# A planner that treats GpSimd and two-operand VectorE work as exclusive, and that waits for work due sooner

## The chip, the core and the metric

The kernel runs on one core of a Trainium2 chip. The metric is device time in microseconds (us), the median of several runs. Five engines run side by side, each through its own queue in order: the tensor engine (PE, with its weight loads PEld), VectorE (DVE), ScalarE (ACT), GpSimd (POOL) and SyncE (SP), which issues the loads and stores here. They wait for each other by semaphores.

## What is computed

One transformer block with normalization behind each half, in float32, for two sequences of 512 tokens of width 512. Attention has 32 query heads and 8 key heads of 128, so that four query heads share a key head; a feed-forward network of inner width 1376 with integer weights and scales per column follows.

```python
q = _rmsnorm((x @ Wq.T).reshape(b, s, 32, 128).transpose(0, 2, 1, 3), q_norm_w)
k = _rmsnorm((x @ Wk.T).reshape(b, s, 8, 128).transpose(0, 2, 1, 3), k_norm_w)
v = (x @ Wv.T).reshape(b, s, 8, 128).transpose(0, 2, 1, 3)
scores = jnp.einsum('bkgqd,bksd->bkgqs', qg, k) / math.sqrt(HD)
bias = jnp.where(rel > 0, NEG_INF, slopes[:, :, None, None] * rel)
attn = jax.nn.softmax(scores + bias[None], axis=-1)
out = jnp.einsum('bkgqs,bksd->bkgqd', attn, v)   # heads joined, then @ Wo.T
x = _layernorm(x + attention(x))
h = silu((x @ gate_w.T) * gate_s) * ((x @ up_w.T) * up_s)
x = _layernorm(x + (h @ down_w.T) * down_s)
```

## The kernel before

**Two halves of a program.** The function post_ln_block does not emit instructions as it goes. It describes operations with `W.add`: their possible engines with a price in us for each (costs), a due time (prio, smaller is sooner), the buffers read and written, and a function that emits the instructions. At the end `W.emit` walks through a simulated time and emits all operations in one order. That order is the program order of each engine's queue, and it also fixes which engine takes an operation that can go to several. Buffers come from rings; an operation that opens a new buffer has to wait in the plan until the users of the buffer it replaces have finished. LAG is what the plan adds from the end of an operation to its visibility on another engine.

**How it chooses.** Before, each step looked at every ready operation on every engine that it may use and took the smallest of (start, due time, end, number), where start is the later of the operation's readiness and the time at which the engine is free. So an operation that could start a moment earlier went first, however late it was due, and was never held back.

**The prices.** `pe(n)` is n/600 us for n columns; `act(n)`, `dve(n)`, `pool_tt(n)` and `pool_ts(n)` are straight lines in the elements per partition. `dve(n, sbuf=True)`, 0.2 + 0.0014 n, was for VectorE work with two operands in SBUF, 0.15 + 0.00106 n for the rest.

**The stages.** Attention is done in units (g, b, i): key head g, sequence b, block i of 128 query tokens; two units make a pair p, and there are 32 pairs. For pair p, with u = 2p, the due times are:
- u - 3: `sums_q`, the sums of a group's weights (tile tq), and `sums_x` of the input (sx), each four additions or subtractions (`sums_a`, `sums_b`); a matrix product is done with seven block products instead of eight (`seven`), which needs such sums of both factors. `sums_o` does the same for the output weights (to), due at u + 1.
- u - 2.4: `project`, the products for queries, keys and values into PSUM banks pa_q, pb_q, pc_q, and their eviction into c: the first value of a block is copied (ACT or DVE), the next is added (DVE).
- u - 1.8: `heads`: squares on ACT (sq), their sum on DVE (ms), the inverse root on POOL (inv, a power of -0.5 of 128x10 values, line 504), the scaling of q and k with it (sq, DVE or POOL), transposes on PE (ptq, ptk), evictions into qT and kT.
- u + k for unit k of the pair: `scores`: for each of four blocks of 32 queries of the four heads, a product on PE (sc), bias and maximum on DVE (pr, nmax), exp on ACT; then the reciprocal of the sums (rden) and four scalings of pr on POOL (line 924).
- u + k + 0.4: `attend`: transposes of pr (pt), evictions (prT), the product with v (pa), its eviction (aT).
- u + 2.6: `project_out`: four sums of aT (so, 128x256 each), seven products with the output weights (pa_o, pb_o, pc_o), each added to y on DVE.

A group's bias is four operations on POOL. After the last group come the first layernorm and the FFN: integer weights are converted to float (wf), summed (sw), multiplied (pa_h, pb_h, pc_h), and `finish` makes sigmoid (ACT) and two products with three factors each (sg, hT, DVE, lines 1289 and 1298). The down projection uses sums of hT (sh) and of its weights (td) and adds to y; the second layernorm and the store follow.

**Sums by either engine.** The helper `tensor` gives an operation to DVE or POOL where both are allowed. Line 518 is therefore the line of all sums and additions in the trace; their tile tells them apart. Line 566 is that of all seven-product matmuls, 641 and 643 are the copies.

Of the kernel before, what the change touches and what calls it, by code (L numbers as in the profile page):

```python
# [53 lines left out]
def act(n, scaled=False):  # L54
    return 0.15 + 0.00084 * n + (0.1 if scaled else 0.0)


def dve(n, sbuf=False):
    return 0.2 + 0.0014 * n if sbuf else 0.15 + 0.00106 * n


def pool_tt(n):
    return 0.28 + 0.0021 * n


def pool_ts(n):
    return 0.3 + 0.00095 * n


LAG = {"PE": 0.22, "DVE": 0.1, "ACT": 0.12, "POOL": 0.2, "SP": 0.1, "ACTQ": 0.1, "NONE": 0.0}  # L70
TABLE = 1.28


class Ring:
# [21 lines left out]
class Work:  # L96
# [3 lines left out]
        self.ops = []  # L100
        self.wrote, self.read = {}, {}

    def add(self, costs, prio, fn, reads=(), writes=(), after=(), table=None, lag=0.0):

        op = {
            "costs": costs,
            "prio": prio,
            "fn": fn,
            "deps": set(id(o) for o in after),
            "obj": list(after),  # L110
            "takes": [],
            "end": None,
            "table": table,
            "lag": lag,
            "n": len(self.ops),
        }
        deps = {id(o): o for o in after}
        for key in reads:
            o = self.wrote.get(key)
            assert o is not None, (key[0].name, key[1])  # L120
            deps[id(o)] = o
        for key in writes:
            o = self.wrote.get(key)
            if o is not None:
                deps[id(o)] = o
            for o in self.read.get(key, ()):
                deps[id(o)] = o
        for key in reads:
            if key not in writes:
                self.read.setdefault(key, []).append(op)  # L130
        for key in writes:
            self.wrote[key] = op
            self.read[key] = []
        bufs = []
        for key in list(reads) + list(writes):
            b = key[0]
            if b not in bufs:
                bufs.append(b)
        for b in bufs:
            op["takes"].append(b)  # L140
            b.users.append(op)
        op["deps"] = list(deps.values())
        self.ops.append(op)
        return op

    def emit(self):
        ops = self.ops
        left = [len(o["deps"]) for o in ops]
        nexts = [[] for _ in ops]
        for o in ops:  # L150
            for d in o["deps"]:
                nexts[d["n"]].append(o)
        free, table = {}, [None]
        dma = 0.0
        ready = []

        def at(o):
            t = 0.0
            for d in o["deps"]:
                t = max(t, d["end"] + d["lag"])  # L160
            return t

        for o in ops:
            if not left[o["n"]]:
                o["at"] = 0.0
                ready.append(o)
        emitted = 0
        while ready:
            best = None
            for o in ready:  # L170
                t0 = o["at"]
                for b in o["takes"]:
                    if b.tile is not None:
                        continue
                    r = b.ring
                    if r.gate is not None and r.gate["end"] is None:
                        t0 = None
                        break
                    k = len(r.items) - r.bufs
                    if k >= 0:  # L180
                        for u in r.items[k].users:
                            if u["end"] is None:
                                t0 = None
                                break
                            t0 = max(t0, u["end"] + LAG[u["eng"]])
                        if t0 is None:
                            break
                if t0 is None:
                    continue
                for e, c in o["costs"].items():  # L190
                    s = max(t0, free.get(e, 0.0))
                    key = (s, o["prio"], s + c, o["n"])
                    if best is None or key < best[0]:
                        best = (key, o, e, c, s)
            assert best is not None, "no work can start: " + ", ".join(
                b.name for o in ready for b in o["takes"]
            )
            _, o, e, c, s = best
            ready.remove(o)
            if e == "ACT" and o["table"] and o["table"] != table[0]:  # L200
                table[0] = o["table"]
                c += TABLE
            o["eng"] = e
            if e in ("SP", "ACTQ"):
                free[e] = s + 0.45
                dma = max(dma, s + 1.6) + c
                o["end"] = dma + 0.6
            elif e == "NONE":
                o["end"] = s
            else:  # L210
                free[e] = s + c
                o["end"] = s + c
            o["lag"] += LAG[e]
            for b in o["takes"]:
                if b.tile is not None:
                    continue
                b.ring.items.append(b)
                b.tile = b.ring.pool.tile(
                    b.ring.shape, b.ring.dtype, tag=b.ring.name, name=b.name, bufs=b.ring.bufs
                )  # L220
            o["fn"](e)
            emitted += 1
            for x in nexts[o["n"]]:
                left[x["n"]] -= 1
                if not left[x["n"]]:
                    x["at"] = at(x)
                    ready.append(x)
        assert emitted == len(ops)
# [3 lines left out]
def post_ln_block(  # L232
# [278 lines left out]


    def tensor(n, prio, dst, a, b, alu, reads, writes, who=("DVE", "POOL"), sbuf=None, after=()):
        cost = {"DVE": dve(n, len(who) > 1 if sbuf is None else sbuf), "POOL": pool_tt(n)}
        W.add(
            {e: cost[e] for e in who},
            prio,
            lambda e: vec[e].tensor_tensor(dst(), a(), b(), alu),  # L518
            reads,
            writes,  # L520
            after,
        )

    def sums_a(n, prio, s, a, s_key, a_keys):
# [113 lines left out]
    def copy_op(n, prio, dst, src, reads, writes, who=("ACT", "DVE")):  # L638
        def fn(e):
            if e == "ACT":  # L640
                nc.scalar.copy(dst(), src())  # L641
            else:
                vec[e].tensor_copy(dst(), src())  # L643

        cost = {"ACT": act(n), "DVE": dve(n), "POOL": 0.2 + 0.00095 * n}
        W.add({e: cost[e] for e in who}, prio, fn, reads, writes)

    def project_plain(p, prio):
# [393 lines left out]
    def layernorm(t, prio, dst, dst_keys, name):  # L1042
        stats, mv = Buf(r_stats, f"stats_{name}"), Buf(r_mv, f"mv_{name}")
        ve, rstd = Buf(r_ve, f"ve_{name}"), Buf(r_rstd, f"rstd_{name}")
        for n in range(2):
            W.add(
                {"DVE": dve(WO)},
                prio,
                lambda e, n=n: nc.vector.bn_stats(stats[:, n, :], y[:, t, n * WO : (n + 1) * WO]),
                [(y, (t, n))],  # L1050
                [(stats, n)],
            )
        W.add(
            {"DVE": 0.2},
            prio,
            lambda e: nc.vector.bn_aggr(mv.tile, stats.tile),
            [(stats, 0), (stats, 1)],
            [A(mv)],
        )
        W.add(  # L1060
            {"DVE": 0.16},
            prio,
            lambda e: nc.vector.tensor_scalar_add(ve.tile, mv[:, 1:2], LN_EPS),
            [A(mv)],
            [A(ve)],
        )
        rsqrt(lambda: rstd.tile, lambda: ve.tile, 1, prio, A(rstd), A(ve))
        W.add(
            {"DVE": 0.6},
            prio,  # L1070
            lambda e: nc.vector.tensor_scalar(
                dst(), y[:, t, :], mv[:, 0:1], rstd.tile, ALU.subtract, ALU.mult
            ),
            [A(mv), A(rstd), (y, (t, 0)), (y, (t, 1))],
            dst_keys,
        )

    x1T, tx = {}, {}
# [40 lines left out]
    for p in range(NP):  # L1119
        g, b, i = pairs[p]  # L1120
        u = 2 * p
# [100 lines left out]
    def ffn_up(fc, b, weights, prio):  # L1222

        fw = min(P, DFF - fc * P)
        key = f"{fc}_{b}"
# [49 lines left out]
        def finish():  # L1275
# [8 lines left out]
                table="sigmoid",  # L1284
# [6 lines left out]
                ),  # L1291
                [(gu, 0), (gu, 1), A(gs_sb), A(sg)],
                [A(sg)],
            )
            W.add(
                {"DVE": 0.75},
# [8 lines left out]
                ),  # L1305
                [(gu, 2), (gu, 3), A(us_sb), A(sg)],
                [(h, (fc, 0)), (h, (fc, 1))],
            )
            finished.append(W.ops[-1])

# [23 lines left out]
    n = 0  # L1334
# [9 lines left out]
    for fc in range(NF):  # L1344
# [22 lines left out]
            sbuf=True,  # L1367
# [138 lines left out]
```

## Time and profile before

| | |
|---|---|
| median of 3 runs | 1091.03 us (1090.96 to 1091.54) |
| profiled execution, its own time | 1091.2 us |
| its span, first to last instruction | 1089.1 us |
| mean granted clock of the tensor engine | 0.997 |
| instructions | 13052 |
| bytes moved by DMA | 38.92 MB |
| POOL scaling of pr, line 924 | x256, 155.8 us busy, mean 627 ns |
| POOL inverse root, line 504 (inv) | x32, 62.9 us busy, mean 1965 ns |
| DVE sums so from aT, 128x256 | x39, 411 / 428 / 870 ns (least, median, most) |
| DVE sums tq from w and tq, 128x768 | x8, 1039 / 2452 / 2464 ns |
| POOL sums tq from w and tq, 128x768 | x12, 1800 / 1812 / 2415 ns |
| DVE scaling sq, 128x640 | x55, 810 / 825 / 1883 ns |

An engine's busy time is the union of its instructions' records. In the rows above, the least duration is that of an operation which ran undisturbed, the greatest that of one which was held up while it was in its engine. A row of waits reads: who waited, on whom, the total, how often, the longest. A matmul in float32 appears as two records; records overlap, since a matmul is given a start and a modelled end, so the starts tell more than the busy time.

### The profile page before, as it was taken

How to read it: one execution, taken by the hardware profiler on the slowest of the kernel's cores; microseconds unless marked ns; L12 is line 12 of the kernel's file. 1: busy time of each engine (PE TensorE's matmuls, PEld its weight loads, DVE VectorE, ACT ScalarE, POOL GpSimd, SP SyncE). 2: the span in 40 equal slices, each digit the busy share in tenths (PEclk: the TensorE clock that was granted, in tenths of full speed). 3: DMA queues.
4: the chain of work that ended last, by engine and by line, in shares of the span. 5: the costliest groups of instructions: out<-in, count | busy, mean ns of one | idle time of the engine just before them, and what ended most of it. 6: DMA issues, size and time to landing. Idle time of an engine off the chain costs nothing.

```text
span 1089.1 us, 13052 instructions
## 1 busy us (share of the span) xinstructions
PE 1070.1 (98%) x4548; PEld 762.2 (70%) x4548; DVE 670.2 (62%) x1563; ACT 411.4 (38%) x1017; POOL 481.3 (44%) x600
## 2 busy tenths in 40 slices
PE   8999999999999999999999999999999999999997
PEld 5667676767676767676766666666666778887886
DVE  7756565656564656465656565657585666677554
ACT  2543334434434343444333434344444434433100
POOL 9444444344534453444344435454573443245130
PEclk9999999999999999999999999999999999999999
DMA  8210011001100120011001100100101013220011
GB/s 280 79 46 14 1 39 59 1 1 40 59 0 1 39 59 1 1 39 59 1 1 40 58 1 1 39 1 1 39 1 29 12 39 97 73 85 20 1 39 39
DMA packets 44144, 38.92 MB, mean 36 GB/s; under 512 B 3664, under 2 KB 36432, under 8 KB 44080
## 3 DMA queue, kind: packets, MB, share of 16 engines
q1 hardware_dynamic: 42352, 37.05, 11.0%
q10 hardware_dynamic: 1728, 1.05, 0.4%
q8 instruction: 36, 0.59, 0.2%
q14 instruction: 28, 0.23, 0.1%
HBM read 35.99 MB, written 2.10 MB: 35 GB/s over the span
## 4 chain that ended last, share of the span: by engine, by line
PE 86%; DVE 5%; POOL 5%; DMA 2%; ACT 1%; issue 1%; SPq 0%; POOLq 0%; DVEq 0%; ACTq 0%
PE pa_q L566 13%; PE pa L966 10%; PE sc L875 10%; PE pa_o L566 9%; PE pa_h L566 6%; PE pt L943 6%; PE pb_q L566 6%; PE pb_o L566 5%; PE pc_q L566 4%; PE pa_d L566 3%; PE pb_h L566 3%; PE ptq L822 2%; DVE tq L518 2%; PE pc_o L566 2%; POOL inv L504 2%; POOL pr L924 2%
## 5 line engine op out<-in xcount | busy, mean ns | idle before, releaser
L924 POOL TENSOR_SCALAR pr<-pr,rden 128x32 f32<-128x32 f32 (+15 forms) x256 | 155.8, 627 | 148.6 <-DVE rden L915 148.0
L900 ACT ACTIVATE pr<-pr,nmax 128x32 f32<-128x32 f32 (+15 forms) x256 | 131.9, 516 | 95.4 <-DVE nmax L884 95.2
L966 PE MATMUL pa<-prT,v 128*128 128x512 f32 x320 | 164.2, 595 | 0.0
L875 PE MATMUL sc<-kT,qT 128*128 128x160 f32 (+15 forms) x512 | 148.9, 402 | 0.0
L884 DVE CUSTOM_DVE_ANT_0 pr<-sc,bias 128x32 f32<-128x32 f32 (+15 forms) x256 | 108.9, 436 | 28.0 <-PE sc L875 25.3
L875 PEld LDWEIGHTS sc<-kT,qT 128*128 128x128 f32 x512 | 90.2, 190 | 47.8 <-issue 29.6
L641 ACT COPY c<-pa_q 128x384 f32<-128x384 f32 x101 | 48.3, 478 | 135.3 <-PE pa_q L566 130.4
L943 PEld LDWEIGHTS pt<-ident,pr 128*128 128x128 f32 x640 | 76.4, 141 | 26.7 <-issue 9.7
L943 PE MATMUL pt<-ident,pr 128*128 128x128 f32 x640 | 91.5, 275 | 0.9 <-POOL pr L924 0.3
L566 PE MATMUL pa_q<-tq,sx 128*128 128x384 f32 x248 | 90.4, 487 | 1.4 <-POOL pr L924 1.4
L641 ACT COPY prT<-pt 128x512 f32<-128x512 f32 x107 | 60.5, 587 | 79.1 <-PE pt L943 78.9
L504 POOL TENSOR_TENSOR inv<-ms,nhalf 128x10 f32<-128x10 f32 x32 | 62.9, 1965 | 53.4 <-DVE ms L780 53.2
L518 DVE TENSOR_TENSOR y<-y,pa_o 128x256 f32<-128x256 f32 x128 | 53.6, 419 | 50.7 <-PE pa_o L566 49.9
L643 DVE COPY prT<-pt 128x512 f32<-128x512 f32 x53 | 36.2, 690 | 61.8 <-PE pt L943 61.7
L764 ACT ACTIVATE sq<-c 128x640 f32<-128x640 f32 x64 | 47.2, 737 | 69.1 <-DVE c L518 67.3
L518 DVE TENSOR_TENSOR c<-pb_q,c 128x384 f32<-128x384 f32 x62 | 34.3, 554 | 61.9 <-PE pb_q L566 58.1
L966 PEld LDWEIGHTS pa<-prT,v 128*128 128x128 f32 x320 | 56.6, 190 | 22.0 <-issue 4.9
L643 POOL COPY v<-c 128x128 f32<-128x128 f32 x50 | 16.0, 321 | 124.1 <-DVE c L518 124.1
L566 PE MATMUL pa_o<-to,so 128*128 128x256 f32 x256 | 65.8, 380 | 0.3 <-POOL pr L924 0.3
L566 PEld LDWEIGHTS pa_q<-tq,sx 128*128 128x128 f32 x248 | 45.9, 192 | 27.5 <-POOL pr L924 2.6
L566 PEld LDWEIGHTS pa_o<-to,so 128*128 128x128 f32 x256 | 47.0, 190 | 20.2 <-issue 9.9
L641 ACT COPY gu<-pa_h 128x256 f32<-128x256 f32 (+1 forms) x88 | 32.1, 370 | 71.5 <-PE pa_h L566 54.8
(152 smaller groups left out, 2048.3 us busy)
## 6 DMA issues: line engine op xcount, KB each, us to landing
w<-in_wqt_dram SPq DMA_DIRECT2D x32, 256.0 KB, 4.2
wo<-in_wot_dram SPq DMA_DIRECT2D x8, 1024.0 KB, 5.5
wi<-in_gwt_dram SPq DMA_DIRECT2D x14, 256.0 KB, 2.8
wi<-in_uwt_dram SPq DMA_DIRECT2D x14, 256.0 KB, 3.2
wdi<-in_dwt_dram SPq DMA_DIRECT2D x10, 256.0 KB, 3.3
y<-in_x_dram SPq DMA_DIRECT2D x1, 2048.0 KB, 12.9
out_dram<-o SPq DMA_DIRECT2D x8, 256.0 KB, 2.0
w<-in_wkt_dram SPq DMA_DIRECT2D x7, 256.0 KB, 4.9
```

The costliest lines, as they stand in the source:

```text
L504: lambda e: nc.gpsimd.tensor_tensor(dst(), src(), nhalf[:, :n], ALU.pow),
L518: lambda e: vec[e].tensor_tensor(dst(), a(), b(), alu),
L566: nc.tensor.matmul(bank[:rows, :width], lhsT=a(fa, c), rhs=b(fb, c), start=(fresh and c == 0), stop=(c == depth - 1), skip_group_check=True,)
L641: nc.scalar.copy(dst(), src())
L643: vec[e].tensor_copy(dst(), src())
L764: lambda e, r=r: nc.scalar.activation(sq[:, r].rearrange("p h d -> p (h d)"), c(r)[:, : 5 * HD], AF.Square),
L875: lambda e, a=a, w=w, sc=sc: nc.tensor.matmul(sc[:, :w], lhsT=qT[:, a, :, :], rhs=kT[:, :w], start=True, stop=True),
L884: lambda e, a=a, w=w, sc=sc: nc.vector.tensor_tensor_reduce(out=pr[:, a, :w], in0=sc[:, :w], in1=bg[:, S - w :], scale=-1.0, scalar=MAX_IN ...
L900: lambda e, a=a, w=w: nc.scalar.activation(pr[:, a, :w], pr[:, a, :w], AF.Exp, bias=nmax[:, a : a + 1], scale=-1.0, accum_out=den[:, a : a ...
L924: lambda e, a=a, w=w: nc.gpsimd.tensor_scalar(pr[:, a, :w], pr[:, a, :w], rden[:, a : a + 1], 1.0, ALU.mult, ALU.mult),
L943: nc.tensor.transpose(pt[:, ts(a, P)], pr[:, a, ts(j, P)], ident.tile)
L966: lambda e, j=j, prT=prT: nc.tensor.matmul(po.tile, lhsT=v[:, j, :], rhs=prT.tile, start=(j == 0), stop=(j == i)),
```

## The change

All of it lies in the planner and in what it is told. No operation is added or removed.

- The price of VectorE work is one line for all kinds, 0.15 + 0.00106 n; the prices of POOL work change by some per cent.
- `add` takes a flag `port`. It is set for the operations of `tensor` that may go to either engine (and the scaled down-weights), for the layernorm's last step and for the FFN's two three-factor products. In the plan, no POOL operation starts before the last marked DVE operation has ended, and no marked DVE operation before the last POOL operation has ended.
- For each engine the best operation is found first. On DVE, ACT and POOL the plan then looks for operations that are due more than HASTE = 0.3 sooner and start less than PATIENT = 0.7 of the first one's duration after it; if there are any, it takes the one of them that starts first. Of the engines' choices the smallest is emitted.
- MARGIN multiplies the prices of all engines but PE; it is 1.

```diff
-def dve(n, sbuf=False):
-    return 0.2 + 0.0014 * n if sbuf else 0.15 + 0.00106 * n
+def dve(n):
+    return 0.15 + 0.00106 * n
 def pool_tt(n):
-    return 0.28 + 0.0021 * n
+    return 0.27 + 0.00197 * n
 def pool_ts(n):
-    return 0.3 + 0.00095 * n
+    return 0.27 + 0.00083 * n
...
+PATIENT = {"DVE": 0.7, "ACT": 0.7, "POOL": 0.7}
+HASTE = 0.3
+MARGIN = 1.0
...
         emitted = 0
+        port = {"DVE": 0.0, "POOL": 0.0}
...
         while ready:
-            best = None
+            at_engine = {}
             for o in ready:
...
                 for e, c in o["costs"].items():
                     s = max(t0, free.get(e, 0.0))
-                    key = (s, o["prio"], s + c, o["n"])
-                    if best is None or key < best[0]:
-                        best = (key, o, e, c, s)
+                    if e == "POOL":
+                        s = max(s, port["DVE"])
+                    elif e == "DVE" and o["port"]:
+                        s = max(s, port["POOL"])
+                    at_engine.setdefault(e, []).append((s, o["prio"], s + c, o["n"], c))
...
+            best = None
+            for e, found in at_engine.items():
+                first = min(found)
+                if e in PATIENT:
+                    s, prio, end = first[:3]
+                    sooner = [
+                        f for f in found if f[1] < prio - HASTE and f[0] < s + PATIENT[e] * (end - s)
+                    ]
+                    if sooner:
+                        first = min(sooner, key=lambda f: (f[0], f[1]))
+                if best is None or first < best[0]:
+                    best = (first, e)
...
                 free[e] = s + c
                 o["end"] = s + c
+                if e == "POOL" or (e == "DVE" and o["port"]):
+                    port[e] = s + c
...
     def tensor(n, prio, dst, a, b, alu, reads, writes, who=("DVE", "POOL"), sbuf=None, after=()):
-        cost = {"DVE": dve(n, len(who) > 1 if sbuf is None else sbuf), "POOL": pool_tt(n)}
+        cost = {"DVE": dve(n), "POOL": pool_tt(n)}
...
+            port=len(who) > 1 if sbuf is None else sbuf,
...
-        cost = {"ACT": act(n), "DVE": dve(n), "POOL": 0.2 + 0.00095 * n}
+        cost = {"ACT": act(n), "DVE": dve(n), "POOL": 0.18 + 0.00086 * n}
...
             dst_keys,
+            port=True,
...
                 [A(sg)],
+                port=True,
...
                 [(h, (fc, 0)), (h, (fc, 1))],
+                port=True,
```

More of the change, by code (lines that the diff above doesn't have):

```diff
@@ L101, in __init__, with add @@
         self.wrote, self.read = {}, {}
-    def add(self, costs, prio, fn, reads=(), writes=(), after=(), table=None, lag=0.0):
+    def add(self, costs, prio, fn, reads=(), writes=(), after=(), table=None, lag=0.0, port=False):
         op = {
-            "costs": costs,
+            "costs": {e: c if e in ("PE", "NONE") else c * MARGIN for e, c in costs.items()},
             "prio": prio,
@@ L114, in add @@
             "lag": lag,
+            "port": port,
             "n": len(self.ops),
@@ L167, in emit, with room @@
         emitted = 0
+        port = {"DVE": 0.0, "POOL": 0.0}
+        def room(o):
+            t = o["at"]
+            for b in o["takes"]:
+                if b.tile is not None:
+                    continue
+                r = b.ring
+                if r.gate is not None and r.gate["end"] is None:
+                    return None
+                k = len(r.items) - r.bufs
+                if k >= 0:
+                    for u in r.items[k].users:
+                        if u["end"] is None:
+                            return None
+                        t = max(t, u["end"] + LAG[u["eng"]])
+            return t
         while ready:
-            best = None
+            at_engine = {}
             for o in ready:
[L171 to L187, printed above, removed]
+                t0 = room(o)
                 if t0 is None:
@@ L191, in emit @@
                     s = max(t0, free.get(e, 0.0))
-                    key = (s, o["prio"], s + c, o["n"])
-                    if best is None or key < best[0]:
-                        best = (key, o, e, c, s)
-            assert best is not None, "no work can start: " + ", ".join(
+                    if e == "POOL":
[3 more added lines that the diff above has]
+                    at_engine.setdefault(e, []).append((s, o["prio"], s + c, o["n"], c))
+            assert at_engine, "no work can start: " + ", ".join(
                 b.name for o in ready for b in o["takes"]
             )
-            _, o, e, c, s = best
+            best = None
[10 more added lines that the diff above has]
+                    best = (first, e)
+            (s, _, _, n, c), e = best
+            o = ops[n]
             ready.remove(o)
@@ L212, in emit @@
                 o["end"] = s + c
+                if e == "POOL" or (e == "DVE" and o["port"]):
+                    port[e] = s + c
+            o["start"] = s
             o["lag"] += LAG[e]
```

## The prediction

> **What bounds the kernel now.** I read the page's first part, then a table of busy time over five stretches, then the waits of the tensor engine, then the timeline around its recurring waits.
>
> ```profile
> PE 1070.1 (98%) x4548; PEld 762.2 (70%) x4548; DVE 670.2 (62%) x1563; ACT 411.4 (38%) x1017; POOL 481.3 (44%) x600
> ...
> PE 86%; DVE 5%; POOL 5%; DMA 2%; ACT 1%; issue 1%; SPq 0%; POOLq 0%; DVEq 0%; ACTq 0%
> ```
>
> These are busy time by engine and the shares of the chain that ended last. The tensor engine (PE) sets the time. The chain leaves it for 14% of the span, but only because it follows the last releaser; most of those detours overlap matmuls.
>
> ```profile
> 0.00:54.50 54.50, 49.70 (x185) 31.85 (x186) 40.48 (x78) 20.16 (x49) 38.39 (x54) 1.00 0.56 179
> 54.50:844.00 789.50, 786.42 (x3313) 536.11 (x3312) 476.83 (x1181) 324.07 (x815) 358.33 (x453) 1.00 0.08 23
> 844.00:1010.00 166.00, 161.36 (x736) 134.05 (x735) 115.07 (x221) 64.58 (x148) 70.78 (x82) 0.99 0.19 54
> 1010.00:1083.10 73.10, 72.58 (x320) 60.15 (x318) 35.65 (x80) 2.56 (x5) 13.29 (x13) 1.00 0.06 22
> 1083.10:1089.10 6.00, 0.00 (x0) 0.00 (x0) 2.12 (x6) 0.00 (x0) 0.55 (x1) 0.68 0.23 87
> ```
>
> Columns: stretch, length, busy PE, PEld, DVE, ACT, POOL, clock, DMA share, GB/s. PE's recorded idle time is 19.0 us: 4.8 at the start, 3.1 in attention, 4.6 in the FFN's first half, 0.5 in its second, 6.0 after the last matmul. That understates it, because a matmul's record runs on after the next could have begun. So I took the starts of the 4548 matmul records and compared each step with columns/1.2 ns. The columns alone make 1037.2 us. The steps exceed this by 44.4 us: 15.2 in excesses of at most 60 ns, mostly a few ns each (256 columns step 216 ns, not 213), and 29.2 us in larger ones, which are stalls. By stage: 2.95 before 8 us (first loads, cold clock), 4.16 at 8 to 31, 0.17 at 31 to 54.5, 13.76 in attention, 7.35 at 844 to 1010, 0.79 after. Only 26.2 us of the 1089.1 can thus be won by any order of work: 29.2 less 2.95.
>
> ```profile
> PE pa_h L566 <- ACT gu L641: 4.6, 4, 2.5
> PE ptq L822 <- DVE sq L518: 2.5, 3, 2.1
> PE pa_q L566 <- POOL pr L924: 1.4, 2, 0.7
> ```
>
> These are PE's longest waits (total us, times, longest). Each ends with an engine that was late itself. The timeline shows why:
>
> ```profile
> 178.63 2.59 POOL L518 TENSOR_TENSOR tq<-w 128x768 f32<-128x768 f32 x1 [4.11 <-PE pa_q L566]
> ...
> 179.57 2.46 DVE L518 TENSOR_TENSOR tq<-w,tq 128x768 f32<-128x768 f32 x1
> ...
> 181.96 0.55 DVE L518 TENSOR_TENSOR c<-pb_q,c 128x384 f32<-128x384 f32 x1
> ...
> 183.30 1.49 DVE L773 TENSOR_REDUCE ms<-sq 128x10 f32<-128x1280 f32 x1 [0.55 <-ACT sq L764]
> ...
> 185.34 1.96 POOL L504 TENSOR_TENSOR inv<-ms,nhalf 128x10 f32<-128x10 f32 x1 [1.19 <-DVE ms L780]
> ```
>
> The same DVE form takes 0.96 alone; the old plan charges 1.28. Beside POOL it takes 2.46. The addition of c, whose matmuls end at 180.7 (start 179.25, 1.46 long), waits in DVE's order until 181.96; squares, mean, inverse root and the scaling of pr all follow late. PE then waits for pr eight times around 189 to 190. This returns about every 107 us, from 609 us on every 54, where a group's weight sums are made; a weaker form without them lies between.
>
> **What the skill says.** "SBUF — State Buffer", Who interferes with whom: a DVE instruction with two SBUF inputs contends with a GpSimd instruction that reads SBUF, and the second to issue blocks until the first finishes. The trace agrees for long operands (2.46 against 0.96). It doesn't for the inverse root:
>
> ```profile
> 292.94 1.96 POOL L504 TENSOR_TENSOR inv<-ms,nhalf 128x10 f32<-128x10 f32 x1
> ...
> 294.15 0.75 DVE L518 TENSOR_TENSOR so<-aT 128x256 f32<-128x256 f32 x2
> ```
>
> Two sums ran inside it at 0.42 each, their time alone; I count 13 such sums inside six of the 32 inverse roots, none stretched. "Perfetto Trace Analysis", Identifying the Most-Contended Engine: matmul busy time is a poor measure of headroom; the trace agrees: of the 29.2 us of stalls only 11.7 (19.0 less 1.3 before the first matmul and 6.0 after the last) are recorded as idle. "TensorE: Matmul & The Clock Gate", Back-to-back issue gap: columns/2.4 + 2.5 ns for one pass; here a 256-column record steps 216 ns, columns/1.2 + 2.7, so the small excess is not a matter of order.
>
> **The change part by part.** No instruction's work or count changes; order on PE, DVE, ACT and POOL, and the choice of DVE or POOL (DVE or ACT for evictions), do. SP's loads follow the same rules as before, at the times that the new plan gives; they land 2 to 13 us after issue and only the first ones are waited for on PE (0.2), so I cost their moves at nothing; if a group's weights came late this would cost up to the 5 us of a landing once.
>
> (a) New prices. POOL 128x768 was 1.89, becomes 1.78, measured 1.81 alone. DVE 128x256 from SBUF was 0.56, becomes 0.42, measured 0.42. POOL scaling of 512 was 0.79, becomes 0.70, measured 0.69. They match operations that run alone, so they are only right with (b).
>
> (b) Exclusion. The plan now puts POOL work and marked DVE work one after the other. DVE's durations in the trace exceed their own undisturbed values by about 60 us in the marked operations, and POOL's scaling of pr by 35 us. This is time DVE stands in front of evictions of PSUM; in the plan it becomes time in which DVE is given unmarked work. At 179.5 the second tq would go first or wait, c could be added at about 180.9 instead of 181.96, and the chain to pr gains about 1 us, the size of the usual stall (ten of the page's forty slices have 1.3 to 1.8 us of excess where their neighbours have 0.4, about 10 of the 13.76). Not all goes: POOL's own queue (tq, inv, four pr) is late next. Bounds: nothing to all 13.76. I take half, -6.9. In the FFN, the gap at 980.3 to 982.9 stands behind sh, sw and td sums of 2.05, 1.10 and 1.75 on DVE where 0.8 and 0.4 would do, and the clock falls afterwards. Bounds: 0 to -7.35; a third, -2.4, because sg and the gate's buffer stay single. Start, 8 to 31 us: mutual blocking again (sx 2.03, sq 1.88), but the loads pace it: 0 to -4.2, I take -1.0.
>
> (c) Patience. DVE, ACT or POOL may stand idle for up to 0.7 of an operation's time if work due over 0.3 sooner will be ready. A waiting POOL tq (1.78) can so be held 1.25 us; behind it stand the group's other sums, due latest and without a waiter for a whole pair, so cover is ample. On DVE, a held operation of 0.42 to 0.96 costs 0.3 to 0.7 of idle time, hidden by its 38% idle; without that cover it would be evictions on which PSUM banks depend. No separate gain is counted: (b)'s halves include it. Cost between nothing and 3 us; with (d).
>
> (d) What the exclusion gets wrong. All 32 inverse roots, 62.9 us, are planned as blocking DVE's marked sums, though the trace shows them harmless. If the so sums of the pair before must come after, they are up to 1.97 us later. Lower bound nothing (other work is ready), upper one so sum of 0.42 per pair, 13.4. I take a quarter of one, 0.1 x 32 = +3.2, for (c) and (d) together.
>
> Sum: -6.9 - 2.4 - 1.0 + 3.2 = -7.1 against the profiled execution's own 1091.2 (span 1089.1 and 2.1 around it): 1084.1. The median, 1091.03, is 0.2 below it, so I say 1084.
>
> **Rivals.** Nearly all stalls go: three quarters of 13.76 and 7.35 and a quarter of 4.16, -16.9: 1074. For it: their common cause is what the plan now knows. Against: a greedy order that is right in durations still has two long POOL queues.
> Nothing: the same stalls move elsewhere, within 2 us: 1091. For it: PE was 98% busy and only 8.2 us of its recorded idle lies between 31 us and the last matmul. Against: the stalls counted by starts are nearly three times as large there (22.1).
> Slower: (d) decides. The four so sums of each pair stand behind the inverse root in the plan; pa_o is late. One ready product (four passes, 1.29 us) covers part of 1.97, leaving 0.68. In three pairs of four this is 16.3, less the 10.3 won: +6, 1097. It outweighs the gain from 15 such pairs on (10.3/0.68); with two ready products nothing is lost. For it: PE has no slack and any new order is felt. Against: the planner sees its own late sums and gives PE other work.
>
> **How the numbers follow.** Forecast 0.46 (about 1079 to 1089), nearly all gone 0.14, nothing 0.12, slower 0.28. The range reaches from 1073 to 1098: the big gain in, all but the far end of the slower case too (all 32 pairs: 21.8 - 10.3, 1102.5). The forecast's own range is 1079 to 1089. 0.2%, 2.2 us, is what a measurement of this kernel can tell from no change. Faster: 0.14, nearly all of the forecast, a little of nothing, 0.60; same 0.12; slower 0.28.
>
> **What would show it.** Right: marked DVE sums near 0.42 and 0.96, first scalings of pr no longer two to five times their own time; starts of matmuls in 54 to 844 us exceed their columns by some 7 us less; POOL busy below 481. Wrong: stretched sums that remain (b fails), or sums gone to their own time while PE's waits for so, ptq or prT rise (d). If POOL and DVE no longer overlap but the span stands, waits have only moved.

## The result and the profile after

The changed kernel takes 1088.87 us (median of 12 runs, 1087.24 to 1090.7); the kernel before took 1092.34 in the 12 runs beside it. The ratio is 0.9971, with a 95% interval of 0.9962 to 0.9981: 3.2 us faster, where 7.1 were forecast. The profiled execution of the changed kernel took 1089.78 with a span of 1088.0. That is only 1.4 us less than the profiled execution before (1091.2), so the account by stage below explains the difference of these two executions, and not the whole difference of the medians.

First the page of the changed kernel: busy time by engine, then the chain that ended last.

```profile
PE 1067.1 (98%) x4548; PEld 763.5 (70%) x4548; DVE 620.8 (57%) x1530; ACT 432.1 (40%) x1049; POOL 447.2 (41%) x601
...
PE 94%; DVE 2%; DMA 2%; POOL 1%; ACT 0%; SPq 0%; issue 0%; POOLq 0%; ACTq 0%
```

DVE is 49 us less busy and POOL 34 us less, while ACT is 21 us more busy: the work as a whole is the same, but DVE has 33 instructions fewer and ACT 32 more. Most of the fall on DVE is blocking which left its records. Measured by how far DVE's durations exceed their undisturbed values (the tenth percentile of the same line, output tile and shape), it went from about 69 us to 26. PE was on the chain for 86% and is now for 94%. Yet PE is 98% busy as before: the share of the chain tells who was late, not how much time that cost.

The busy time over the same five stretches as before, changed kernel (length, busy PE, PEld, DVE, ACT, POOL, clock, DMA share, GB/s):

```profile
0.00:54.50 54.50, 51.03 (x184) 32.71 (x185) 32.95 (x74) 22.59 (x55) 32.31 (x54) 1.00 0.57 179
54.50:844.00 789.50, 785.61 (x3333) 539.39 (x3332) 443.05 (x1167) 345.85 (x850) 332.30 (x455) 1.00 0.08 23
844.00:1010.00 166.00, 159.49 (x722) 132.25 (x721) 107.95 (x206) 60.80 (x141) 61.03 (x73) 0.99 0.18 52
```

In attention PE has 3313 matmul records before and 3333 now in the same 789.5 us: it is ahead by 20. In the third stretch it loses 6.5 us idle, where it lost 4.6, and falls behind by 14. PE's waits of the changed kernel, the longest four:

```profile
PE pa_h L594 <- ACT gu L669: 5.1, 1, 5.1
PE pb_q L594 <- DVE c L545: 1.9, 1, 1.9
PE warm L454 <- POOL ident masks.py:199: 1.3, 1, 1.3
PE pa_q L594 <- ACT c L669: 1.2, 2, 0.6
```

Two single waits have taken the place of many. The measure of the prediction (steps from one matmul's start to the next, above columns/1.2 ns, steps with over 60 ns of excess) gives the account by stage. All figures are us of one profiled execution:

| stretch | before | changed |
|---|---|---|
| 0 to 54.5 (start) | 7.3 | 7.6 |
| 54.5 to 109 | 0.5 | 3.0 |
| 109 to 790 (attention, regular part) | 11.5 | 2.2 |
| 790 to 844 | 1.7 | 4.9 |
| 844 to 900 (FFN begins) | 2.9 | 9.4 |
| 900 to 978 | 0.0 | 0.0 |
| 978 to 1010 | 4.5 | 0.0 |
| 1010 to the end | 0.8 | 0.8 |
| sum | 29.2 | 27.9 |

13.8 us were won in two stretches, and 12.5 given back in four others. The first of the two large waits begins so in the changed kernel's timeline (DVE, ACT and PE; start, length, instruction):

```profile
889.81 2.04 DVE L545 TENSOR_TENSOR tx<-x1T 128x512 f32<-128x512 f32 x2 [0.23 <-ACT x1T L669]
890.30 0.36 ACT L669 COPY gu<-pa_h 128x256 f32<-128x256 f32 x1
891.77 1.41 DVE L545 TENSOR_TENSOR tx<-x1T,tx 128x512 f32<-128x512 f32 x2
893.09 0.74 DVE L1318 SCALAR_TENSOR_TENSOR sg<-gu,gs_sb,sg 128x512 f32<-128x512 f32 x1
893.87 0.75 DVE L1328 SCALAR_TENSOR_TENSOR hT<-gu,us_sb,sg 128x512 f32<-128x512 f32 x1
...
894.72 0.37 ACT L669 COPY gu<-pa_h 128x256 f32<-128x256 f32 x1 [4.06 <-DVE hT L1328]
...
895.11 2.05 PE L594 MATMUL pa_h<-tx,sw 128*128 128x256 f32 x4 [5.08 <-ACT gu L669]
```

DVE took the four sums tx of the second sequence's input as soon as the last copy into x1T was done. ACT had finished the sigmoid at 890.39, but the gate's products sg and hT waited behind tx; ACT could not evict into gu until hT had been done; PE had no free bank. These tx sums inherit the due time of the layernorm (64.8), sooner than that of the waiting gate products (67), but no product that is due before 72 reads them. At 798 us the same four sums of the first sequence stand in front of the addition of c from pb_q: PE's other long wait.

### The profile page after: what moved, and what is told of

Its sections match the earlier page's. It is cut to its first block, busy times and chain, and to the rows that moved or that the text cites. A ratio compares the mean times of both kernels' runs of the same rounds, so it can differ in the third digit from the quotient of the medians.

```text
span 1088.0 us, 13048 instructions
## 1 busy us (share of the span) xinstructions
PE 1067.1 (98%) x4548; PEld 763.5 (70%) x4548; DVE 620.8 (57%) x1530; ACT 432.1 (40%) x1049; POOL 447.2 (41%) x601
## 4 chain that ended last, share of the span: by engine, by line
PE 94%; DVE 2%; DMA 2%; POOL 1%; ACT 0%; SPq 0%; issue 0%; POOLq 0%; ACTq 0%
PE pa_q L594 14%; PE pa L994 13%; PE sc L903 11%; PE pa_o L594 10%; PE pb_q L594 7%; PE pa_h L594 7%; PE pt L971 6%; PE pb_o L594 5%; PE pc_q L594 4%; PE pb_h L594 3%; PE pa_d L594 3%; PE ptq L850 2%; PE pc_o L594 2%; PE pc_h L594 2%; PE pb_d L594 2%; PE pc_d L594 1%
## 5 line engine op out<-in xcount | busy, mean ns | idle before, releaser
L952 POOL TENSOR_SCALAR pr<-pr,rden 128x32 f32<-128x32 f32 (+15 forms) x256 | 121.1, 492 | 146.5 <-DVE rden L943 145.4
L971 PE MATMUL pt<-ident,pr 128*128 128x128 f32 x640 | 85.5, 273 | 0.0
L669 ACT COPY aT<-pa 128x512 f32<-128x512 f32 x59 | 34.5, 585 | 69.3 <-PE pa L994 69.3
L594 PEld LDWEIGHTS pa_o<-to,so 128*128 128x128 f32 x256 | 46.6, 191 | 18.4 <-DVE y L545 6.1
```

Source lines behind the costliest of these rows:

```text
L594: nc.tensor.matmul(bank[:rows, :width], lhsT=a(fa, c), rhs=b(fb, c), start=(fresh and c == 0), stop=(c == depth - 1), skip_group_check=True,)
L952: lambda e, a=a, w=w: nc.gpsimd.tensor_scalar(pr[:, a, :w], pr[:, a, :w], rden[:, a : a + 1], 1.0, ALU.mult, ALU.mult),
L971: nc.tensor.transpose(pt[:, ts(a, P)], pr[:, a, ts(j, P)], ident.tile)
```

## Experiments

The plan can be read before anything runs: in the planned order of PE, I added up the times between one operation's planned end and the next one's planned start, and the 0.9 us before the first. This sum, the plan's own idle time, is 19.6 us in the kernel before and 18.4 in the changed one, whose plan already holds a wait of 5.4 us at the FFN's begin and one of 2.1 at pb_q. Theory A is that the chip pays the plan's idle time, plus what the plan doesn't know. Theory B is that patience alone causes the new waits; theory C that patience, not the exclusion, removed the old ones. Every ratio is to the kernel before, on the same chip.

**Exclusion without patience.**

```diff
-PATIENT = {"DVE": 0.7, "ACT": 0.7, "POOL": 0.7}
+PATIENT = {}
```

> The change without patience: new prices and the exclusion alone. Theory A (the exclusion's plan fits the chip, so the tensor engine's idle time that the plan itself holds is what comes back; the plan's idle between consecutive tensor-engine operations adds up to 27.6 us here, 18.4 in the changed kernel, 19.6 in the one before): about 9 us slower than the changed kernel, a ratio to the one before of 1.003 to 1.008, with one stall of about 1 us per half group between 109 and 790 us again. Theory B (patience alone causes the new stalls at the passages between stages, and the exclusion is the pure gain): faster than the changed kernel, ratio 0.990 to 0.995, the stalls at about 798 and 895 us gone and those between 109 and 790 us still at about 2 us in all.

Ratio 1.0005 (0.9995 to 1.0015), 1091.76 us: short of A's range, but far from B's. Between 109 and 790 us stalls of 9.4 us remain, and those of 54.5 to 109 and of 790 to 844 us, 3.4 and 7.1, are larger than in the changed kernel. The waits of PE for rden in the first row, about 1.1 us late each, lie at 249, 463, 571 and 847 us, so they are fewer than one per half group:

```profile
PE pa L994 <- DVE rden L943: 3.5, 4, 0.9
PE pt L971 <- POOL pr L952: 2.7, 4, 1.5
PE ptq L850 <- DVE sq L545: 2.6, 1, 2.6
```

B is half right all the same. From 844 to 900 us only 1.9 us are lost instead of 9.4, so the large wait there does need patience; but patience is also what clears the regular part while the exclusion is drawn as it is.

**Patience alone, at the old prices.** The exclusion is taken out of the changed kernel, and its prices are put back to those before:

```diff
-                    if e == "POOL":
-                        s = max(s, port["DVE"])
-                    elif e == "DVE" and o["port"]:
-                        s = max(s, port["POOL"])
...
-def dve(n):
-    return 0.15 + 0.00106 * n
+def dve(n, sbuf=False):
+    return 0.2 + 0.0014 * n if sbuf else 0.15 + 0.00106 * n
```

> Patience alone: the old prices, no exclusion. Theory A: the plan is still blind to the mutual blocking, so stalls that it doesn't hold remain; its own idle is 19.0 us, close to the 19.6 of the kernel before, so a ratio of 0.997 to 1.004, with stretched sums (tq and so of DVE far over 0.96 and 0.42 us) still there and more than 8 us of stalls between 109 and 790 us. Theory C (patience is what removed the stalls of the attention stage): those between 109 and 790 us at 2 to 4 us, ratio 0.997 or below, as in the changed kernel.

Ratio 0.9985 (0.9978 to 0.9992). The regular part of attention loses only 3.6 us, which C expected, not A; sums are stretched as before and the ratio lies in A's range and outside C's. Where the kernel before added c at 181.96 us, behind two tq sums of DVE, this one adds it at 179.13, ahead of DVE's tq at 182.23. The wait at the FFN's begin is there without any exclusion, and it begins in the same way; timeline of this kernel:

```profile
887.42 0.69 DVE L544 TENSOR_TENSOR tx<-x1T 128x512 f32<-128x512 f32 x1 [0.40 <-ACT x1T L668]
...
888.14 2.77 DVE L544 TENSOR_TENSOR tx<-x1T,tx 128x512 f32<-128x512 f32 x2
...
890.83 1.21 DVE L1317 SCALAR_TENSOR_TENSOR sg<-gu,gs_sb,sg 128x512 f32<-128x512 f32 x1
...
893.80 1.65 PE L593 MATMUL pb_h<-tx,sw 128*128 128x256 f32 x3 [6.17 <-POOL sw L544]
```

Here tx even shared POOL and DVE, and DVE again left its gate for it; PE's wait ends with a weight sum on POOL that was late itself. This kernel differs from the one before in patience alone, and the FFN's begin (844 to 900 us) loses 9.5 us where it lost 2.9. So patience is enough for this wait, without any exclusion.

**The inverse roots taken out of the exclusion.** The operation of `rsqrt` carries a mark, and POOL's start and port skip it:

```diff
-                    if e == "POOL":
+                    if e == "POOL" and not o.get("free"):
...
-                if e == "POOL" or (e == "DVE" and o["port"]):
+                if (e == "POOL" and not o.get("free")) or (e == "DVE" and o["port"]):
```

> The changed kernel, but the plan no longer takes POOL's inverse roots as excluding DVE's marked sums. Theory A (step d of the prediction: the exclusion is drawn too wide): the plan's idle falls from 18.4 to 13.1 us, the chip follows because sums ran inside inverse roots at their time alone, ratio 0.991 to 0.994. Theory B (it is patience, not the width of the exclusion): ratio within 0.002 of the changed kernel's 0.9971. If inverse roots do exclude sums, sums beside them are stretched and the ratio is 0.998 or above.

Ratio 0.9903 (0.9888 to 0.9918), 1080.81 us: 7.4 us better than the changed kernel (0.0068 of 1092), somewhat more than A's range. Timeline of this kernel:

```profile
187.41 1.97 POOL L531 TENSOR_TENSOR inv<-ms,nhalf 128x10 f32<-128x10 f32 x1
...
187.62 0.75 DVE L546 TENSOR_TENSOR so<-aT 128x256 f32<-128x256 f32 x2
...
188.29 0.42 DVE L546 TENSOR_TENSOR so<-so,aT 128x256 f32<-128x256 f32 x1
...
188.75 0.42 DVE L546 TENSOR_TENSOR so<-aT,so 128x256 f32<-128x256 f32 x1
```

All four sums of a pair run inside one inverse root at their time alone. In the changed kernel one such sum did so in the whole run, before it 13. Theory B falls, and so does the idea that roots exclude sums. The mark of `rsqrt` also spares the 16 smaller roots of the layernorms (128x1, about 0.55 us each), which lie in the passages; what share of the gain is theirs was not separated.

**The same without patience.** Both edits together.

> Exclusion without the inverse roots, and no patience. The plan's own idle is 5.6 us. Theory A (plan and chip agree): 12 to 13 us below the changed kernel, ratio 0.985 to 0.988. If patience is needed on the chip because real durations scatter: no better than the roots-free kernel with patience, ratio 0.991 or above.

Ratio 0.9839 (0.9824 to 0.9855), 1073.73 us: 14.4 us below the changed kernel, where A expected 12 to 13, and far from its rival. Patience, which helped the wide exclusion by 3.7 us (1.0005 to 0.9971), costs 7.0 once the exclusion is right (0.9839 to 0.9903).

**Prices alone, and prices with patience.** Each leaves out the exclusion and keeps the new prices; the first (prices alone) is without patience too:

```diff
-                    if e == "POOL":
-                        s = max(s, port["DVE"])
-                    elif e == "DVE" and o["port"]:
-                        s = max(s, port["POOL"])
...
-PATIENT = {"DVE": 0.7, "ACT": 0.7, "POOL": 0.7}
+PATIENT = {}
```

> The new prices alone: no exclusion, no patience. The plan's own idle of the tensor engine is 7.4 us, but its prices are those of work that runs alone and it lets POOL and marked DVE work run side by side. Theory A (a plan pays for what it doesn't know): sums are stretched as before (DVE's excess again 50 us or more), stalls of 8 us or more between 109 and 790 us, ratio to the kernel before 0.996 to 1.006. Rival (the blocking matters little, prices and any new order suffice): ratio 0.990 or below.

> The change without its exclusion: new prices and patience. The plan's own idle is 11.3 us against 18.4 in the changed kernel. Theory A (the exclusion as drawn costs what it does at the inverse roots and gains elsewhere): unplanned blocking adds 4 to 8 us, ratio 0.994 to 1.000, near the changed kernel's 0.9971. Rival (the exclusion as drawn is nothing but a cost): ratio 0.992 or below.

Ratios 0.9970 (0.9957 to 0.9983) and 1.0033 (1.0021 to 1.0044). The first is as good as the whole change, though it knows nothing of blocking; its regular part loses 6.6 us, under the 8 expected, and DVE's durations exceed their undisturbed values by about 60 us, as expected. Its rival, that prices and any new order suffice, would have needed 0.990. The second is worse than A's range: its plan holds 11.3 us of idle time and its execution shows 33.9 us of stalls, of which these are the longest waits:

```profile
PE pa_h L593 <- DVE sw L544: 6.2, 1, 6.2
PE pa_q L593 <- DVE c L670: 4.2, 1, 4.2
```

The likely reading is that a plan with true prices but no exclusion is tight where the chip blocks, and that patience then waits for work that comes late. The rival, that the exclusion as drawn is only a cost, falls beside patience, where the exclusion wins 6.8 us (1.0033 to 0.9971). Without patience it is true: the exclusion as drawn costs 3.8 us there (0.9970 to 1.0005), and one that spares the inverse roots wins 14.3 (0.9970 to 0.9839).

**A later due time for tx**, in the changed kernel:

```diff
             sums_b(
                 2 * NTH,
-                prio,
+                (NU + 2.0, NU + 7.0)[b],
```

> The changed kernel with another due time for the sums tx of the normed input (66 for the first sequence, 71 for the second, where they were 58.8 and 66.8), so that patience no longer puts them before the addition of c and before the gate's products. Theory A (the two new stalls come from patience and these due times): the stall at about 798 us (2.0 us and the slowed clock after it) goes, that at about 895 us falls from 5.3 to about 3.4, ratio 0.991 to 0.994. Rival (they come from the exclusion): both stay, ratio 0.996 to 0.998.

Ratio 0.9910 (0.9894 to 0.9927), 1082.00 us. The wait at 798 us is gone (790 to 844: 4.9 to 1.1 us); the FFN's begin loses 5.5 instead of 9.4, in a wait of 2.7 us. Both go as A expected and the gain, 6.7 us, is at its upper end. (The due times before were 56.8 and 64.8; the expectation gives them 2 too high.) So the due time of the tx sums alone is worth twice the whole change here.

**All three: roots free, no patience, later due time.**

> Exclusion without the inverse roots, no patience, and the later due time for tx. The plan's own idle is 4.0 us against 5.6 in the roots-free kernel without patience, which had a ratio of 0.9839. Theory A: the stalls of 844 to 978 us (2.5) fall by half, ratio 0.981 to 0.984. If due times matter only to patience: 0.984.

Ratio 0.9805 (0.9785 to 0.9825), 1070.41 us: faster than both kernels, a little better than A's range, and better than the 0.9839 without the new due time. The rival, that due times matter only to patience, falls: without patience this one is still worth 3.7 us by the ratios, 1.9 us of it in the stalls of the two profiled executions. Busy time by stretch, columns as above:

```profile
0.00:54.50 54.50, 50.17 (x198) 32.78 (x198) 37.19 (x83) 21.59 (x51) 35.94 (x57) 1.00 0.55 179
54.50:844.00 789.50, 789.50 (x3355) 542.89 (x3355) 447.88 (x1185) 341.36 (x849) 356.69 (x473) 1.00 0.08 23
844.00:1010.00 166.00, 166.00 (x767) 141.12 (x767) 107.81 (x219) 60.37 (x134) 42.11 (x51) 1.00 0.18 52
```

From 54.5 to 1010 us PE shows no idle time at all. What stalls are left, 9.5 us, lie for the most part in the start (5.8).

**Patience put back into it.**

> The best kernel so far (roots free, later due time for tx, ratio 0.9805) with patience put back. The plan's own idle is 13.4 us against 4.0. If patience costs by itself, not only through the due times of tx: 8 to 10 us more than without it, ratio 0.988 to 0.991, with a stall of about 3 us where the FFN begins. If those due times were its only fault: 0.980 to 0.983.

Ratio 0.9903 (0.9887 to 0.9920), with a stall of 2.8 us at 887 us. So patience costs by itself, 10.7 us here, and not only through the due times of tx: beside it and free roots, the later due time brings nothing (0.9903 with and without). Five pairs of these kernels differ in patience alone, and in each the FFN's begin (844 to 900 us) loses more with it:

| pair | stalls without patience (us) | with |
|---|---|---|
| old prices | 2.9 | 9.5 |
| new prices | 4.1 | 9.1 |
| exclusion | 1.9 | 9.4 |
| exclusion, roots free | 1.1 | 4.9 |
| the same, tx later | 0.2 | 6.5 |

The limits of patience, 0.7 and 0.3, and patience on one engine alone were not varied.

All kernels side by side, with the plan's idle time and the stalls of over 60 ns in one profiled execution (us):

| kernel | plan's idle | stalls on the chip | ratio |
|---|---|---|---|
| before | 19.6 | 29.2 | 1 |
| old prices, patience | 19.0 | 28.9 | 0.9985 |
| new prices | 7.4 | 27.4 | 0.9970 |
| new prices, patience | 11.3 | 33.9 | 1.0033 |
| exclusion | 27.6 | 32.1 | 1.0005 |
| exclusion, patience (the change) | 18.4 | 27.9 | 0.9971 |
| the change, tx later | 14.5 | 20.3 | 0.9910 |
| exclusion, roots free, patience | 13.1 | 21.0 | 0.9903 |
| the same, tx later | 13.4 | 21.7 | 0.9903 |
| exclusion, roots free | 5.6 | 11.4 | 0.9839 |
| the same, tx later | 4.0 | 9.5 | 0.9805 |

With the exclusion, the chip's stalls exceed the plan's by 4 to 10 us; with true prices and none, by 20 and 23. The old prices, which for long DVE sums lie above the undisturbed time (1.28 against 0.96 us for 768 elements), came within 10 too. The exclusion made a plan with true prices honest. What the plan was then, was not good.

## Why the prediction was right and wrong

**The direction and the bound** were right: PE's stalls, counted by starts, are what an order of work can win, and the best kernel here takes 19 of those 26.2 us.

**Steps (a) and (b)** came true in part. DVE's tq sums of w and tq had a median of 2452 ns, and the POOL scalings a mean of 627; in the changed kernel's answers:

```profile
L545 POOL TENSOR_TENSOR tq<-w,tq x18: 1803/1810/1822, 77.8 to 770.8; 128x768 f32<-128x768 f32 x18
L545 POOL TENSOR_TENSOR tq<-w x11: 1812/2581/2587, 74.2 to 766.1; 128x768 f32<-128x768 f32 x11
...
L545 DVE TENSOR_TENSOR tq<-w,tq x2: 952/952/953, 13.6 to 15.3; 128x768 f32<-128x768 f32 x2
```

```profile
L952 POOL TENSOR_SCALAR pr<-pr,rden 128x32 f32<-128x32 f32 (+15 forms) x256 | 121.1, 492 | 146.5 <-DVE rden L943 145.4
```

Only two of those eight DVE sums are left and take 952, less than the least of 1039 before, so that none of the eight had run undisturbed (the others went to POOL, at 1810), and the mean of 627 has become 492. But POOL's sums tq of w alone have a median of 2581 ns, as they had before. The exclusion sets planned times, and through them the order of each queue; nothing in the program makes POOL wait for DVE. Two sums that the same matmul releases still start side by side, as here in the changed kernel:

```profile
182.19 0.96 DVE L545 TENSOR_TENSOR tq<-w 128x768 f32<-128x768 f32 x1 [0.57 <-PE pa_q L594]
182.24 2.58 POOL L545 TENSOR_TENSOR tq<-w 128x768 f32<-128x768 f32 x1 [5.41 <-PE pa_q L594]
```

The 54.5 to 844 us stretch won 3.7 us where 6.9 were forecast: its regular part won 9.3, more than that, and its two ends lost 5.6. In the FFN the gap near 980 us went entirely (-4.5, of which -2.4 was counted for the whole stage), while its begin lost 6.5. I had looked for cover behind the stalls seen, and never asked what would be late in the passages between stages. The start's -1.0 came where it was forecast: 8 to 31 us has 2.7 us of stalls instead of 4.2. But 0 to 8 lost 1.1 and 31 to 54.5 lost 0.7, so that the whole start is 0.3 worse.

**Step (c)** failed. It says that patience costs between nothing and 3 us, with DVE's 38% idle time as cover. The cover was no cover: the idle time is spread over the run, while the work held up at 890 us was the gate's, with one sg and two gu buffers behind it. The step named evictions as what would suffer, and priced it as if it couldn't happen. Beside the exclusion as drawn, patience wins 3.7 us on the whole, because it also repairs the regular part; with the exclusion right, it costs 7 us, and 10.7 with the later due time.

**Step (d)** named the right fault, seen in the trace before, and sized it too small: 0.1 us per pair, 3.2 in all together with (c). The inverse roots cost 7.4 us beside patience, and 18 without it (1.0005 against 0.9839). Together (c) and (d) cost 14.4 us (0.9839 to 0.9971). The step had this within its bounds (13.4 and 3) and then took a fifth of them for no measured reason. So the failed term of the sum is the +3.2 for (c) and (d), which measured +14.4.

So the sum was -10.3 + 3.2 and the parts are -17.6 and +14.4: the gain of (a) and (b) was under-sized as well, and the two errors partly cancelled, which was luck. I had taken half of attention's stalls and a third of the FFN's where an order without these two faults removes most of them. The nearly-all rival's 1074 is what the roots-free kernel without patience reached (1073.73). That 9.3 us came from 109 to 790 us is shown; that they came from the exclusion, as step (b) has it, isn't: patience alone at old prices brings 7.9 of them, the exclusion as drawn without patience 2.1, and the exclusion with the roots free and without patience all 9.3.

**The slower rival** had the mechanism of (d) in the wrong place. The so sums did leave the inverse roots, but beside patience the regular part lost nothing by it (2.2 us of stalls; without patience 9.4, and 2.2 with the roots free): the cost came up in the passages. Compared with the kernel that differs in the roots alone (roots free, patience), the changed kernel has 2.7 us more stalls at 54.5 to 109 us, 2.0 more at 790 to 844, 4.5 more at 844 to 900, and 2.5 fewer in the regular part. How each root there turns into a wait was not traced further.

## What to carry to other kernels

A planner's rule that is right (two engines exclude each other) pays only as far as it is drawn where the hardware has it, so test its exceptions in a trace first: here one exempted kind of operation was worth two to six times the whole change. A rule that waits for what is due sooner makes due times binding, so check them before adding it; here better due times did not make it pay. And read the idle time of the bounding engine out of the plan before running it: with true prices and the exclusion in the plan, as drawn or with the roots free, the chip paid what the plan held and 4 to 10 us more.

## What the runs showed of the hardware

An inverse root on POOL (128x10, 1.97 us) doesn't hold up a two-operand DVE sum: in the best kernel 29 of them ran inside one, 26 so sums at 387 to 426 ns and three of to at 683 to 691, all at their time alone. The Trainium skill, "SBUF — State Buffer", Who interferes with whom, lets whoever issues first block the other for the whole instruction; for this one the measurement decides otherwise, while POOL's sums of 768 elements agree with it (2.58 us beside a DVE sum of 0.96 that started 0.05 us sooner, 1.81 alone). The other way round, a sum does hold up a root that starts while it runs: such a root took 2359 ns in the kernel with new prices alone, where a sum to had 514 ns left to run, and 2152 in the best kernel, where a sum so had 323 left. Both fit a root that shuts out sums only at its start, perhaps because it reads only ten values per partition; that is a guess, and other operations of this kind were not tried.

The two long waits of PE in the changed kernel cost more than their length. After 1.9 us of recorded idle time at 796.7, two 384-column steps of the changed kernel from 799.43 on took 640 ns instead of 322 and two 416-column ones 693 instead of 349; full speed was back at 802.8, and the steps since 798.58 add up to 1.8 us over their columns. After the 5.1 us at 895, six 256-column steps took 413 to 427 ns instead of 216. The changed kernel's timeline shows it in four records before and four after that wait:

```profile
888.99 1.03 PE L594 MATMUL pb_h<-tx,sw 128*128 128x256 f32 x4
...
895.11 2.05 PE L594 MATMUL pa_h<-tx,sw 128*128 128x256 f32 x4 [5.08 <-ACT gu L669]
```
